# Attention on one Trainium2 core: PSUM as a ring of eight single banks, one exp per head, repeated transfers for the split rows

## The chip, the cores and the metric

The kernel runs on one NeuronCore of a Trainium2 chip. The metric is the device time of one launch in microseconds, from repeated runs; the profile is that of one further execution.

The engines named below are TensorE (PE in the profile; PEld is its weight load), VectorE (DVE), ScalarE (ACT), GpSimd (POOL) and SyncE (SP), whose list here only issues transfers. A transfer is issued by SP, by ACT or by POOL, each in the order of its own list.

## The reference

One transformer block with conditioning, on x of shape 2 x 2048 x 576 in float32, with 16 heads of 36 dimensions and an MLP of 2304:

```python
mod = jax.nn.silu(c) @ w_ada + b_ada
sh_msa, sc_msa, g_msa, sh_mlp, sc_mlp, g_mlp = jnp.split(mod, 6, axis=1)
xn = _ln(x, 1e-06) * (1 + sc_msa[:, None, :]) + sh_msa[:, None, :]
qkv = (xn @ w_qkv + b_qkv).reshape(B, N, 3, H, hd)
q, k, v = (qkv[:, :, 0], qkv[:, :, 1], qkv[:, :, 2])
q = _ln(q, 1e-05, qn_g, qn_b)
k = _ln(k, 1e-05, kn_g, kn_b)
attn = jnp.einsum('bqhd,bkhd->bhqk', q, k) * hd ** (-0.5)
attn = jax.nn.softmax(attn, axis=-1)
o = jnp.einsum('bhqk,bkhd->bqhd', attn, v).reshape(B, N, C) @ w_proj + b_proj
x = x + g_msa[:, None, :] * o
xn2 = _ln(x, 1e-06) * (1 + sc_mlp[:, None, :]) + sh_mlp[:, None, :]
x = x + g_mlp[:, None, :] * (jax.nn.gelu(xn2 @ w1 + b1, approximate=False) @ w2 + b2)
```

## The kernel before

For each of the two batch entries b the kernel first makes q, k and v for 16 tiles of 128 tokens (`inputs`, L360 and L371 the matmuls), normalises q and k per head, and transposes them to feature-major rows: `qo` holds q's five chunks of 128 features (and the first rows of k), `kr` the rest of k. Then comes `attend`, then the projection (`outputs`). After both entries come the two products of the MLP.

`attend` runs over head pairs p (8), query blocks qb of 512 tokens (4) and key groups g (4): 128 steps for each b. A step works on two heads and on two halves of the keys, which makes four row groups of 32 partitions, so that four small matmuls run side by side in TensorE. A head has 36 dimensions, and a row group takes 32: the first 32 ("main", tiles km and qm) go as float32, two passes each, and the last four ("ends", ke and qe) as 16 rows, in which each of the four dimensions stands four times as high and low part[...]. `parted` splits the copies on VectorE into high and low parts (L767, L768), with masks by partition (low and sign).

In a step, `scores` makes two rounds, one for each of two blocks of 128 keys: four main matmul pairs and four ends matmuls (L974) into two PSUM tiles of two banks each, the two heads side by side; then an exp of 128x1024 for each tile (L979) into one of five `pt` buffers. `values` then multiplies the probabilities of the step before with v (L988, 16 matmul records), both heads into one bank, and VectorE moves this sum into `ot` (L1034 for the first key group, L1036 adds the others). v has a column of ones, so one row of the sum is the denominator. So TensorE's order is scores of step n, values of step n - 1, scores of step n + 1, and so on; the loop writes this order out, and VectorE's order is also that of the code.

PSUM has eight banks of 512 float32 per partition. They are one pool of four two-bank tiles (`s_tile`), used in turn by everything. A step of attention takes four for scores and one for the sum, of which the sum uses one bank.

Work that isn't due at once stands in `later`, a list of lists that is popped once a step: `take_q` issues the transfers of q for the next query block at once and splits the ends two steps on; `take_k` does so for the next head pair's keys four steps on; `finish` sends the denominators to memory and back (L1003, L1004), and `divided` takes the reciprocal (L1007), scales (L1008) and sends the head's rows back into `qo` (L1013) three steps on. All of these transfers are on SP's list. `rows_taken` issues, for each of the four row groups, one or two transfers of main rows (L755) and four of the same four rows of ends (L758).

`hooks` places other work at named steps: transposes of the last two token tiles (`last_inputs`) at the first four steps of each b, and for b = 0 the gates and the MLP's modulation from w_ada at steps of p = 0, 1 and 2. `outputs` later loads rows of x through GpSimd's list (L1065) into parts of `kr`, as soon as these are free.

Of the kernel before, what the change touches and what calls it, by code (L numbers as in the profile page):

```python
# [8 lines left out]
F32 = mybir.dt.float32  # L9
F32R = mybir.dt.float32r  # L10
I32 = mybir.dt.int32
AF = mybir.ActivationFunctionType
# [4 lines left out]
P = 128  # L17
# [14 lines left out]
def dit_block(  # L32
# [53 lines left out]
    def s_tile():  # L86
        return psum["s"].tile([P, 2, 512], F32, tag="s", name="s")

    def acc_tile():
        return psum["a"].tile([P, 512], F32, tag="acc", name="acc")  # L90

# [6 lines left out]
    def opened_psum(**bufs):  # L98

        stack = ExitStack()  # L100
        for n, count in bufs.items():
            psum[n] = stack.enter_context(
                tc.tile_pool(name=f"ps_{n}", bufs=count, space=PSUM, reuse_waits="tile")
            )
        return stack.close

    def load_rows(dst, w):

# [65 lines left out]
    def ada_rows(was):  # L174


        ps = s_tile()[:, 0, :PART]
        for k in range(NKC):
            kk = P if k < FULL else 64
            for c in range(4):  # L180
                i, a = divmod(c, 2)
                nc.tensor.matmul(
                    ps[32 * c : 32 * c + 32, :],
                    sil[:kk, k, :],
                    was[i][:kk, k, 256 * a : 256 * a + PART],
                    start=(k == 0),
                    stop=(k == FULL),
                )
        return ps
# [25 lines left out]

    def features(rows, whichs):

        tp = s_tile()[:, 0, :384].rearrange("p (s r) -> p s r", s=3)
        for s in range(3):
            nc.tensor.transpose(tp[:, s, :], rows[:, s * P : (s + 1) * P], ident)  # L220
        for i in range(2):
            for a, chunks in enumerate((slice(0, 2), slice(2, 5))):
                n = chunks.stop - chunks.start
                r0 = 32 * (2 * i + a)
                nc.vector.tensor_copy(mod[:, whichs[i], chunks, :], tp[:, :n, r0 : r0 + B])
# [480 lines left out]
    def block_of_small():  # L706
# [25 lines left out]
        high = kv.tile([P, BLK], F32R, name="high")  # L732

        low_k, low_q, sign_k, sign_q = (kv.tile([P, 1], F32, name=f"part{i}") for i in range(4))
        eights = ident.rearrange("p (r a b) -> p r a b", r=4, a=4)[:, :, 1, :]
        fours = ident.rearrange("p (r a b d) -> p r a b d", r=4, a=4, b=2)[:, :, 0:2, 1, :]
        nc.vector.tensor_reduce(low_k, eights, AX.XY, ALU.add)
        nc.vector.tensor_reduce(low_q, fours, AX.XYZ, ALU.add)
        for low, sign in ((low_k, sign_k), (low_q, sign_q)):
            nc.vector.tensor_scalar(sign, low, -2.0, 1.0, ALU.mult, ALU.add)  # L740
        nc.gpsimd.memset(vv[:, :, :, HD : HD + 1], 1.0)
# [4 lines left out]
            return qo[:, c, cols] if c < NKC else kr[:, c - NKC, cols]  # L746


        def rows_taken(main, ends, halves, first, src, dst):

            for c in halves:
                for h in range(2):
                    r0 = 32 * (2 * c + h)
                    for i, row, d, n in head_rows(first + h * HD, DIMS):
                        nc.sync.dma_start(out=main[r0 + d : r0 + d + n, dst], in_=chunk(i, src(c))[row : row + n, :])  # L755
                    ((i, row, _, n),) = head_rows(first + h * HD + DIMS, HD - DIMS)
                    for j in range(4):
                        nc.sync.dma_start(  # L758
                            out=ends[r0 + n * j : r0 + n * j + n, dst], in_=chunk(i, src(c))[row : row + n, :]
                        )  # L760

        def parted(ends, rows, low, sign):

# [8 lines left out]
        def take_k(p):  # L772
            m, e = km[p % 2], ke[p % 2]
            src = lambda c: slice(c * N // 2, (c + 1) * N // 2)
            rows_taken(m, e, range(2), C + p * 2 * HD, src, slice(0, N // 2))
            return lambda: parted(e, slice(0, P), low_k, sign_k)

        def take_k_block(t0, t1):

            c, k0 = divmod(t0 * P, N // 2)  # L780
            dst = slice(k0, k0 + (t1 - t0) * P)
            rows_taken(km[0], ke[0], (c,), C, lambda c: slice(t0 * P, t1 * P), dst)
            return lambda: parted(ke[0][:, dst], slice(64 * c, 64 * c + 64), low_k, sign_k)

        def take_q(p, qb):
            i = qb % 2
            src = lambda c: slice(qb * BLK, (qb + 1) * BLK)
            rows_taken(qm[i], qe[i], range(2), p * 2 * HD, src, slice(0, BLK))
            return lambda: parted(qe[i], slice(0, P), low_q, sign_q)

        def last_chunk(dst, w, groups, f):
# [35 lines left out]
        def inputs(b, weights, work, xnt, loaded):  # L827
# [64 lines left out]
                    taken.append(take_k_block(*key_tiles[i - 1 : i + 1]))  # L892

            def last(t, chunks):
                ps = s_tile()
                by_feature(t, (ps[:, 0], ps[:, 1]), chunks, True)
                left = [*taken]
                taken.clear()
                return left
# [54 lines left out]
        def attend(b, pool, hooks):  # L954
# [5 lines left out]
            def scores(p, qb, g):  # L960
                i, j = p % 2, qb % 2
                pts = []
                for k0 in (2 * g * P, (2 * g + 1) * P):
                    keys = slice(k0, k0 + P)
                    tiles = [s_tile() for c in range(2)]
                    for k, q, first in (
                        (km[i], qm[j], True),
                        (ke[i].bitcast(F32R), qe[j].bitcast(F32R), False),
                    ):
                        for c in range(2):  # L970
                            for h in range(2):
                                r0 = 32 * (2 * c + h)
                                r = slice(r0, r0 + (DIMS if first else 4 * (HD - DIMS)))
                                nc.tensor.matmul(  # L974
                                    tiles[c][:, h, :], k[r, keys], q[r, :], start=first, stop=not first
                                )
                    for c, ps in enumerate(tiles):
                        pt = pool.tile([P, 2, BLK], F32, name="pt", bufs=5)
                        nc.scalar.activation(pt, ps, AF.Exp, scale=SCALE)  # L979
                        pts.append((pt, k0 // P + c * NT // 2))  # L980
                return pts

            def values(p, pts):
                acc = s_tile()[:, 0, :]
                for pt, kc in pts:
                    for h in range(2):
                        v0 = (kc * H + 2 * p + h) * HV
                        nc.tensor.matmul(  # L988
                            acc[64 * h : 64 * h + 64, :],
                            vt[:, v0 : v0 + 64],  # L990
                            pt[:, h, :],
                            start=pt is pts[0][0],
                            stop=pt is pts[-1][0],
                        )
                return acc
# [27 lines left out]
            for p, qb, g in [*steps, (None, None, None)]:  # L1023
                pts = None if p is None else scores(p, qb, g)
                if g == 0 and (p, qb) != (NPAIR - 1, NBLK - 1):
                    later[2].append(take_q(*((p, qb + 1) if qb + 1 < NBLK else (p + 1, 0))))
                if g == 1 and qb == 1 and p + 1 < NPAIR:
                    later[4].append(take_k(p + 1))
                if behind is not None:
                    bp, bqb, bg, bpts = behind  # L1030
                    acc = values(bp, bpts)
                    if bg == 0:
                        ot = pool.tile([P, BLK], F32, name="ot", bufs=2)
                        nc.vector.tensor_copy(ot, acc)  # L1034
                    else:
                        nc.vector.tensor_tensor(ot, acc, ot, ALU.add)  # L1036
                    if bg == NG - 1:
                        later[3].append(finish(bp, bqb, ot))
                if (p, qb, g) in hooks:
                    later[1] += hooks[p, qb, g]() or []  # L1040
                later.append([])
                for do in later.pop(0):
                    do()
                behind = (p, qb, g, pts)
# [82 lines left out]
        for b in range(B):  # L1127
# [2 lines left out]
                last_inputs = inputs(b, weights, work, xnt, loaded)  # L1130
            close_weights()
            att, close_att = opened("att")
            km[1] = att.tile([P, N // 2], F32, name="km1")
            qm[1] = att.tile([P, BLK], F32, name="qm1")
            opening = {}
# [22 lines left out]
            def output_opened():  # L1158
# [2 lines left out]
            hooks = {  # L1161
                (0, 0, 0): lambda: last_inputs(NT - 2, range(NKC - 1, NQK)),
                (0, 0, 1): lambda: last_inputs(NT - 1, range(NKC - 1, NQK)),
                (0, 0, 2): lambda: last_inputs(NT - 2, range(NKC - 1)),
                (0, 0, 3): last_inputs_done,
                (4, 0, 1): output_opened,
            }
            if b == 0:
# [6 lines left out]
            with tc.manual_schedule(engines={mybir.EngineType.DVE}):  # L1175
                attend(b, att, hooks)
            close_att()
            wp, close_wp = opening["wp"]
            if b + 1 < B:
                weights, close_weights = input_weights()  # L1180
# [351 lines left out]
```

## Time and profile before

| | |
|---|---|
| median of 3 runs | 3327.55 us (3326.79 to 3329.52) |
| the profiled execution | 3329.74 us, of which span 3327.5 us |
| granted TensorE clock | 0.994 |
| TensorE busy | 3250.7 us (98%) |
| ScalarE busy | 1440.7 us (43%) |
| VectorE busy | 1457.9 us (44%) |
| GpSimd busy | 255.0 us (8%) |

By stretches of the span: first conditioning to 30 us; q, k and v of b = 0 to 258 us; attention to 1075 us; projection to 1146 us; q, k, v and attention of b = 1 to 2190 us; projection to 2291 us; first MLP product to 2829 us; second to the end. Between 300 and 1075 us TensorE is busy for 761.56 us, ScalarE for 478.16, VectorE for 258.04 and GpSimd for 24.70.

How to read it: a row of a group gives line, engine, operation, output and input tiles with shapes, the count, then busy time and mean nanoseconds of one, then the idle time of the engine just before and what ended it. A float32 matmul shows as two records. The chain of waits gives start, length and what the end of the program was waiting for at that moment; "issue" is time in which the engine waited for nothing that the profile shows. A timeline line gives start, length, engine, line, operation, tiles and, in brackets, the idle time before it with its releaser; SPq is SP's list of transfers.

### The profile page before, as it was taken

How to read it: one execution, taken by the hardware profiler on the slowest of the kernel's cores; microseconds unless marked ns; L12 is line 12 of the kernel's file. 1: busy time of each engine (PE TensorE's matmuls, PEld its weight loads, DVE VectorE, ACT ScalarE, POOL GpSimd, SP SyncE). 2: the span in 40 equal slices, each digit the busy share in tenths (PEclk: the TensorE clock that was granted, in tenths of full speed). 3: DMA queues.
4: the chain of work that ended last, by engine and by line, in shares of the span. 5: the costliest groups of instructions: out<-in, count | busy, mean ns of one | idle time of the engine just before them, and what ended most of it. 6: DMA issues, size and time to landing. Idle time of an engine off the chain costs nothing.

```text
span 3327.5 us, 47009 instructions
## 1 busy us (share of the span) xinstructions
PE 3250.7 (98%) x18143; PEld 1892.2 (57%) x18143; DVE 1457.9 (44%) x2073; ACT 1440.7 (43%) x1928; POOL 255.0 (8%) x249
## 2 busy tenths in 40 slices
PE   8999999999999999999999999998999999999998
PEld 5774333333333777633333333357888788777776
DVE  4664333333333366533333333255455443554554
ACT  2335656666666033356666666633555543000000
POOL 1110000000000211100000000041000000111111
PEclk9999999999999999999999999999999999999999
DMA  3002212212111401021111111144322222523321
GB/s 127 26 27 62 73 44 64 54 45 52 45 44 29 143 26 30 18 57 44 42 42 43 36 44 41 35 169 145 120 84 88 81 81 77 191 100 119 130 100 37
DMA packets 123324, 234.28 MB, mean 70 GB/s; under 512 B 22412, under 2 KB 65365, under 8 KB 121045
## 3 DMA queue, kind: packets, MB, share of 16 engines
q1 hardware_dynamic: 112124, 193.10, 18.8%
q0 software_dynamic: 10240, 36.61, 3.2%
q8 instruction: 146, 2.39, 0.3%
q10 hardware_dynamic: 728, 1.48, 0.1%
q14 instruction: 86, 0.70, 0.1%
HBM read 125.96 MB, written 56.91 MB: 55 GB/s over the span
## 4 chain that ended last, share of the span: by engine, by line
PE 86%; ACT 7%; issue 2%; DMA 2%; DVE 1%; SPq 1%; POOL 0%; ACTq 0%; DVEq 0%; POOLq 0%
PE s L988 28%; PE s L1460 14%; PE s L360 14%; PE s L974 11%; PE m L1310 11%; ACT pt L979 7%; PE m L1324 2%; PE s L371 2%; PE one L1310 2%; PE s L874 1%; DMA wb<-in_w_dram 1%; PE t L1369 1%; SPq L758 0%; PE s L338 0%; DMA qo<-ot 0%
## 5 line engine op out<-in xcount | busy, mean ns | idle before, releaser
L979 ACT ACTIVATE pt<-s 128x1024 f32<-128x1024 f32 x1024 | 994.1, 1024 | 611.2 <-PE s L988 348.0
L988 PE MATMUL s<-pt,vt 128*64 128x512 f32 x4096 | 940.1, 601 | 18.0
L988 PEld LDWEIGHTS s<-pt,vt 128*64 128x64 f32 x4096 | 272.9, 137 | 621.1 <-issue 452.8
L974 PE MATMUL s<-qm,km 32*128 32x512 f32 x4096 | 578.0, 616 | 5.8 <-DVE ot L1034 5.7
L974 PE MATMUL s<-qe,ke 16*128 16x512 f32 x2048 | 430.9, 789 | 5.2 <-DVE ke L768 4.6
L1036 DVE TENSOR_TENSOR ot<-s,ot 128x512 f32<-128x512 f32 x192 | 132.7, 691 | 682.7 <-PE s L988 682.7
L360 PE MATMUL s<-wq,xnt 128*128 128x288 f32 x1536 | 394.2, 412 | 3.6 <-ACT xnt L346 3.6
L974 PEld LDWEIGHTS s<-qm,km 32*128 32x128 f32 x4096 | 193.5, 185 | 280.1 <-ACT pt L979 203.4
L1460 PE MATMUL s<-ws,as 128*128 128x288 f32 x1440 | 351.8, 406 | 0.0
L360 PEld LDWEIGHTS s<-wq,xnt 128*128 128x128 f32 x1536 | 287.1, 191 | 96.0 <-issue 18.5
L1460 PEld LDWEIGHTS s<-ws,as 128*128 128x128 f32 x1440 | 273.6, 190 | 75.6
L1007 DVE RECIPROCAL den<-den 128x512 f32<-128x512 f32 x64 | 213.9, 3343 | 3.8 <-DMA den<-den_dram 3.8
L1310 PE MATMUL m<-xnt,wb 128*128 128x256 f32 x864 | 214.5, 384 | 0.9 <-DVE product L1074 0.9
L1310 PE MATMUL m<-s,wb 128*128 128x256 f32 x864 | 210.2, 379 | 3.1 <-DVE s L1284 3.1
L1034 DVE COPY ot<-s 128x512 f32<-128x512 f32 x64 | 44.2, 691 | 364.6 <-PE s L988 264.3
L974 PEld LDWEIGHTS s<-qe,ke 16*128 16x128 f32 x2048 | 112.0, 185 | 120.6 <-issue 111.9
L1310 PEld LDWEIGHTS m<-s,wb 128*128 128x128 f32 x864 | 164.0, 190 | 26.1 <-DVE s L1284 3.5
L1310 PEld LDWEIGHTS m<-xnt,wb 128*128 128x128 f32 x864 | 159.4, 190 | 33.8 <-issue 12.2
L1337 DVE TENSOR_TENSOR cs<-m,cs 128x512 f32<-128x512 f32 x72 | 49.7, 691 | 233.5 <-ACT cs L1336 157.2
L1460 PE MATMUL s<-ws,hidden 128*128 128x288 f32 x576 | 142.3, 406 | 0.0
L1348 ACT ACTIVATE cs<-cs,b_sb 128x512 f32<-128x512 f32 x144 | 103.9, 722 | 87.4 <-DVE cs L1343 87.4
L1446 DVE TENSOR_TENSOR as<-hidden 128x1152 f32<-128x1152 f32 x80 | 139.5, 1807 | 0.0
(147 smaller groups left out, 2433.2 us busy)
## 6 DMA issues: line engine op xcount, KB each, us to landing
gelu<-cs SPq DMA_DIRECT2D x144, 256.0 KB
hidden<-gelu SPq DMA_DIRECT2D x16, 2304.0 KB
qe<-qo SPq DMA_DIRECT2D x1024, 8.0 KB
den<-den_dram SPq DMA_DIRECT2D x128, 128.0 KB
qm<-qo SPq DMA_DIRECT2D x192, 64.0 KB
xr<-x_dram SPq DMA_DIRECT2D x32, 288.0 KB
out_dram<-y POOLq DMA_DIRECT2D x32, 288.0 KB, 3.7
qo<-ot SPq DMA_DIRECT2D x104, 72.0 KB
```

Source lines behind the costliest of these rows:

```text
L360: nc.tensor.matmul(outs[a], stationary(k, a), moving(k, a), start=(first and k == 0), stop=(not first and k == FULL - 1),)
L371: nc.tensor.matmul(outs[a], stationary(FULL, a)[r], moving(FULL, a)[r], start=first, stop=not first)
L974: nc.tensor.matmul(tiles[c][:, h, :], k[r, keys], q[r, :], start=first, stop=not first)
L979: nc.scalar.activation(pt, ps, AF.Exp, scale=SCALE)
L988: nc.tensor.matmul(acc[64 * h : 64 * h + 64, :], vt[:, v0 : v0 + 64], pt[:, h, :], start=pt is pts[0][0], stop=pt is pts[-1][0],)
L1007: nc.vector.reciprocal(den, den)
L1036: nc.vector.tensor_tensor(ot, acc, ot, ALU.add)
L1310: nc.tensor.matmul(out_m[m], wb[:, slot[m], k, f * P : (f + 1) * P], moving[m](k), start=k == 0 and (m == 1 or (first and m in (2, 5, 6))) ...
L1324: nc.tensor.matmul(out_m[m], w[r, f * P : (f + 1) * P], a[r, FULL, t * PAIR : (t + 1) * PAIR], start=first and m != 4, stop=not first and ...
L1348: nc.scalar.activation(part, part, AF.Gelu, bias=b1_sb[:, g : g + 1])
L1446: nc.vector.tensor_tensor(stationary[m], x_, y_, op)
L1460: nc.tensor.matmul(ms[m], stationary[m][:, f, :], ws[m][:, f, :], start=(f == 0), stop=(f == HF - 1))
```

## The change

In attention, and there alone, PSUM is opened as eight tiles of one bank (`psum["b"]`); `bank()` takes the next of them, or half an `s_tile` where that pool isn't open. Each score matmul group gets a bank of its own and each head an exp of 128x512 into its half of `pt`. The sum takes the ninth bank of a step, which in a ring of eight is the step's first one again.

The four transfers of ends become one whose source repeats each row four times. The copies of a row now lie side by side, not the four rows as blocks, so the masks of the split change. `take_k` issues on GpSimd's list, all else stays on SP's. Two of the four hooks of `last_inputs` move from steps 2 and 3 to steps 4 and 5, and what a hook returns is put ahead of what `later` holds for that step.

```diff
+    def bank():
+        return psum["b"].tile([P, 512], F32, tag="b", name="b") if "b" in psum else s_tile()[:, 0, :]
...
-        eights = ident.rearrange("p (r a b) -> p r a b", r=4, a=4)[:, :, 1, :]
-        fours = ident.rearrange("p (r a b d) -> p r a b d", r=4, a=4, b=2)[:, :, 0:2, 1, :]
-        nc.vector.tensor_reduce(low_k, eights, AX.XY, ALU.add)
-        nc.vector.tensor_reduce(low_q, fours, AX.XYZ, ALU.add)
+        parts = ident.rearrange("p (r a b) -> p r a b", a=2, b=2)
+        nc.vector.tensor_reduce(low_k, parts[:, :, 1, :], AX.XY, ALU.add)
+        nc.vector.tensor_reduce(low_q, parts[:, :, :, 1], AX.XY, ALU.add)
...
-                    for j in range(4):
-                        nc.sync.dma_start(
-                            out=ends[r0 + n * j : r0 + n * j + n, dst], in_=chunk(i, src(c))[row : row + n, :]
-                        )
+                    values = chunk(i, src(c))[row : row + n, :]
+                    queue.dma_start(
+                        out=ends[r0 : r0 + 4 * n, dst],
+                        in_=values.unsqueeze(1).to_broadcast([n, 4, values.shape[1]]),
+                    )
...
-            rows_taken(m, e, range(2), C + p * 2 * HD, src, slice(0, N // 2))
+            rows_taken(nc.gpsimd, m, e, range(2), C + p * 2 * HD, src, slice(0, N // 2))
...
-                    tiles = [s_tile() for c in range(2)]
+                    banks = [bank() for _ in range(4)]
...
-                        for c in range(2):
-                            for h in range(2):
-                                r0 = 32 * (2 * c + h)
-                                r = slice(r0, r0 + (DIMS if first else 4 * (HD - DIMS)))
-                                nc.tensor.matmul(
-                                    tiles[c][:, h, :], k[r, keys], q[r, :], start=first, stop=not first
-                                )
-                    for c, ps in enumerate(tiles):
+                        for r0, ps in zip(range(0, P, 32), banks):
+                            r = slice(r0, r0 + (DIMS if first else 4 * (HD - DIMS)))
+                            nc.tensor.matmul(ps, k[r, keys], q[r, :], start=first, stop=not first)
+                    for c in range(2):
                         pt = pool.tile([P, 2, BLK], F32, name="pt", bufs=5)
-                        nc.scalar.activation(pt, ps, AF.Exp, scale=SCALE)
+                        for h in range(2):
+                            nc.scalar.activation(pt[:, h, :], banks[2 * c + h], AF.Exp, scale=SCALE)
...
-                acc = s_tile()[:, 0, :]
+                acc = bank()
...
-                    later[1] += hooks[p, qb, g]() or []
+                    later[1] = (hooks[p, qb, g]() or []) + later[1]
...
+            close_psum()
+            close_psum = opened_psum(b=8)
...
-                (0, 0, 2): lambda: last_inputs(NT - 2, range(NKC - 1)),
-                (0, 0, 3): last_inputs_done,
+                (0, 1, 0): lambda: last_inputs(NT - 2, range(NKC - 1)),
+                (0, 1, 1): last_inputs_done,
...
             close_att()
+            close_psum()
+            close_psum = opened_psum(s=4)
```

More of the change, by code (lines that the diff above doesn't have):

```diff
@@ L104, in opened_psum, with close @@
             )
-        return stack.close
+        def close():
+            stack.close()
+            for n in bufs:
+                del psum[n]
+        return close
     def load_rows(dst, w):
@@ L174, in ada_rows @@
     def ada_rows(was):
-        ps = s_tile()[:, 0, :PART]
+        ps = bank()[:, :PART]
         for k in range(NKC):
@@ L216, in features @@
     def features(rows, whichs):
-        tp = s_tile()[:, 0, :384].rearrange("p (s r) -> p s r", s=3)
+        tp = bank()[:, :384].rearrange("p (s r) -> p s r", s=3)
         for s in range(3):
@@ L746, in chunk, with rows_taken @@
             return qo[:, c, cols] if c < NKC else kr[:, c - NKC, cols]
-        def rows_taken(main, ends, halves, first, src, dst):
+        def rows_taken(queue, main, ends, halves, first, src, dst):
             for c in halves:
@@ L754, in rows_taken @@
                     for i, row, d, n in head_rows(first + h * HD, DIMS):
-                        nc.sync.dma_start(out=main[r0 + d : r0 + d + n, dst], in_=chunk(i, src(c))[row : row + n, :])
+                        queue.dma_start(out=main[r0 + d : r0 + d + n, dst], in_=chunk(i, src(c))[row : row + n, :])
                     ((i, row, _, n),) = head_rows(first + h * HD + DIMS, HD - DIMS)
-                    for j in range(4):
-                        nc.sync.dma_start(
-                            out=ends[r0 + n * j : r0 + n * j + n, dst], in_=chunk(i, src(c))[row : row + n, :]
-                        )
+                    values = chunk(i, src(c))[row : row + n, :]
[3 more added lines that the diff above has]
+                    )
         def parted(ends, rows, low, sign):
@@ L781, in take_k_block @@
             dst = slice(k0, k0 + (t1 - t0) * P)
-            rows_taken(km[0], ke[0], (c,), C, lambda c: slice(t0 * P, t1 * P), dst)
+            rows_taken(nc.sync, km[0], ke[0], (c,), C, lambda c: slice(t0 * P, t1 * P), dst)
             return lambda: parted(ke[0][:, dst], slice(64 * c, 64 * c + 64), low_k, sign_k)
@@ L787, in take_q @@
             src = lambda c: slice(qb * BLK, (qb + 1) * BLK)
-            rows_taken(qm[i], qe[i], range(2), p * 2 * HD, src, slice(0, BLK))
+            rows_taken(nc.sync, qm[i], qe[i], range(2), p * 2 * HD, src, slice(0, BLK))
             return lambda: parted(qe[i], slice(0, P), low_q, sign_q)
@@ L894, in last @@
             def last(t, chunks):
-                ps = s_tile()
-                by_feature(t, (ps[:, 0], ps[:, 1]), chunks, True)
+                by_feature(t, [bank() for _ in range(0, len(chunks), 4)], chunks, True)
                 left = [*taken]
```

## The prediction

> **What bounds the kernel now.** I read the page first (busy shares, then the chain that ended last), then the rows of the three attention lines, then the chain of waits over a few steps, then the timelines of ScalarE and of SP's queue.
>
> ```profile
> PE 3250.7 (98%) x18143; PEld 1892.2 (57%) x18143; DVE 1457.9 (44%) x2073; ACT 1440.7 (43%) x1928; POOL 255.0 (8%) x249
> PE 86%; ACT 7%; issue 2%; DMA 2%; DVE 1%; SPq 1%; POOL 0%; ACTq 0%; DVEq 0%; POOLq 0%
> L979 ACT ACTIVATE pt<-s 128x1024 f32<-128x1024 f32 x1024 | 994.1, 1024 | 611.2 <-PE s L988 348.0 <-PE s L974 262.3
> L1336 ACT COPY cs<-one 128x256 f32<-128x256 f32 x72 | 26.8, 372 | 172.9 <-PE one L1310 160.5 <-ACT std L265 12.0 <-PE t L1369 0.2
> ```
>
> TensorE counts as busy for 98%, yet the chain that ended last gives ScalarE 7%, all of it in the exps of L979. Ends of matmuls are modelled, so a TensorE that stands still for a fraction of a microsecond can pass for busy. The chain of waits over two attention steps shows where:
>
> ```profile
> 344.28 3.65 PE s L988 x16
> 347.94 1.36 PE s L974 x11
> 349.30 0.00 ACTq L979
> 349.31 0.04 issue
> 349.35 1.03 ACT pt L979
> 350.38 0.04 issue
> 350.43 1.93 PE s L988 x7
> ```
>
> A step (one of 2 x 128) is 3.65 us of L988 (probabilities times values) and two rounds of scores (L974). The next L988 starts only after an exp of 1.03 us. Each step takes five two-bank tiles from a ring of four, so the sum of L988 gets the tile of the step's first score pair, whose exp has just begun. TensorE's timeline, first in this step, then in a step where ScalarE was long done, gives the price:
>
> ```profile
> 349.06 1.04 PE L974 MATMUL s<-qm,km 32*128 32x512 f32 x8
> 349.52 0.81 PE L974 MATMUL s<-qe,ke 16*128 16x512 f32 x4
> 350.43 0.65 PE L988 MATMUL s<-pt,vt 128*64 128x512 f32 x2
> ...
> 1640.54 0.70 PE L974 MATMUL s<-qm,km 32*128 32x512 f32 x2 [0.37 <-DVE ot L1034]
> 1640.55 0.50 PE L974 MATMUL s<-qe,ke 16*128 16x512 f32 x2
> 1641.07 0.59 PE L974 MATMUL s<-qm,km 32*128 32x512 f32 x2
> 1641.10 0.80 PE L974 MATMUL s<-qe,ke 16*128 16x512 f32 x2
> 1641.83 0.65 PE L988 MATMUL s<-pt,vt 128*64 128x512 f32 x2
> ```
>
> From the last "ends" matmuls to L988 it is 0.91 us with the wait and 0.73 us without. Of the 0.17 some 0.03 is the spread of four starts against two, so the exp costs 0.14 us a step, not its whole 1.03.
>
> The second window also shows another wait: L974 waits for DVE's copy into ot (L1034), and that for qo<-ot on SP's queue, which had no free moment before it:
>
> ```profile
> 1624.03 0.54 SPq L755 DMA_DIRECT2D km<-kr  x1
> 1624.61 1.23 SPq L758 DMA_DIRECT2D ke<-kr  x2
> 1625.94 1.80 SPq L755 DMA_DIRECT2D qm<-qo  x3
> 1627.83 7.05 SPq L758 DMA_DIRECT2D qe<-qo  x11
> 1634.98 2.12 SPq L1013 DMA_DIRECT2D qo<-ot  x3
> ```
>
> **The sum wait (each head's exp by itself, sum in the first head's bank).** 1024 exps of 128x1024 become 2048 of 128x512. Their price is not in the trace; the two rows above, PSUM sources at 1024 and 256 elements, give (1024 - 372) / 768 = 0.849 ns an element, so about 590 ns for 512. Three long exps in a row take 2.85 us in ScalarE's timeline, one each 0.91, so neighbours overlap by 0.11: 0.48 us each. The Trainium skill, "ScalarE: Activation LUTs", section "What ACT_TABLE_LOAD costs", states 186 ns plus 0.833 ns an element and an overlap of about 93 ns, so 613 ns and 0.52 us each, which speaks for cutting exps into fewer, longer ones. I take the trace's 0.48 and keep 0.52 as the upper end of the likely.
>
> Does it fit? With five pt buffers, the exps of a step from its third on wait for L988 to free a buffer: the first of them starts 1.19 us after L988 (345.49 or 351.61 in the timeline). Six short exps then end at 1.19 + 5 x 0.48 + 0.59 = 4.18 us (4.40 by the skill's price). Their banks are wanted again by the second round of scores, whose weight loads start at 348.83 - 344.28 = 4.55 and matmuls at 4.78. So it fits by 0.37 or 0.15 us. The sum's bank: its exp starts at 349.35 as before, ends at 349.94 instead of 350.38, and TensorE could take it up at 350.26 at the earliest (349.52 + 0.73). The wait is then hidden by 0.3 us of scores; what is late next is TensorE itself. Gain 0.14 us a step, over the some 230 of 256 steps in which the trace is undisturbed: 32 us. ScalarE's total goes from 4.1 to 4.2 us of a 6.0 us step at most.
>
> **One repeated transfer instead of four.** Each take of q or k issues about 4.75 transfers of main rows and 16 of ends; the ends become 4. The qe issues take 7.05 / 11 = 0.64 us each on SP, so 12 fewer save 7.7 us of SP time per take. A block of four steps (24.6 us) holds about 17.9 us of SP issues in an ordinary stretch (344 to 363: 2.91 + 7.03 + 1.52 + 0.61 + 1.49 + 2.52 + 0.67 + 1.15), and another 13 in the one block per head pair where k is taken, which doesn't fit. Bytes are the same. The price of the repeated transfer is not in the trace: as the four had it at best (0.64 for all, landing 1.63 us as ke<-kr in the chain), as all four in a row at worst (2.6 us), which is no gain. I take the former, since issue time follows the instruction in all these rows (0.54 to 0.8 us for 8 to 128 KB). Low and sign masks change their pattern only: two DVE reductions in set-up, beside DMA, at nothing; without that cover, under 1 us.
>
> **k on GpSimd's queue.** About nine transfers of 0.54 us issue (L1065, two in 1.07 us), 5 us per head pair, on an engine that is 8% busy; landing near 4 us. They pass SP's list of q, den and qo. Behind them on GpSimd stand the memsets for ada and the loads of x for the projection, none due for tens of us; the memsets wait at most for key rows, all written by step 1. Against it speaks "SBUF — State Buffer" in the Trainium skill, section "SBUF: two separate sides": a transfer issued from GpSimd gets no descriptors while DVE holds the port they share. By the trace DVE's longest operation here is the 3.34 us reciprocal (L1007). Were each of nine transfers held by one, it would be 30 us; nothing in the trace says that the reciprocal holds the port. km is free one head pair early, and the split of k on DVE stands nine steps (54 us) behind that: hidden by either price. If it weren't, DVE would stand in its list before an eviction, and TensorE with it.
>
> What the relief of SP is worth: of the 254 gaps between L988 starts most are 6.13 to 6.15 us. Eight, about one per head pair (1.3 us in the window above), are over by 8 in sum; six behind the ada loads (408 to 456 us) by 11. I count 15 of these 19 us, the rest because 18 ada transfers and 2.6 MB of weights stay on SP.
>
> **Start of each half, last rows moved.** The first three gaps of a half are 7.46, 9.89 and 8.31, then 7.45, 10.84 and 8.79 us: 7.2 and 8.7 over. In it TensorE waits for the last keys:
>
> ```profile
> 290.89 0.68 PE L974 MATMUL s<-qe,ke 16*128 16x512 f32 x2 [2.31 <-DVE ke L768]
> 292.94 1.98 PE L988 MATMUL s<-pt,vt 128*64 128x512 f32 x4
> ```
>
> After that pause L988 takes 4.86 us instead of 3.65 (granted clock 0.96 over the stretch). The two heads' keys go through ten transfers (282.13 to 288.6); six fewer and the split placed ahead of q's on DVE bring the keys some 3.7 us earlier, so the 2.3 us pause and most of the 1.2 us behind it go. The transposes of the last q columns only move, from steps 2 and 3 to 4 and 5; with them each half keeps about 2.8 us of transposes. I count 9 of 15.9 us. New pools of PSUM and the close of work two steps later: a handful of waits at the two ends of attention, put at zero, bounds minus and plus 2 us.
>
> **Sum.** 32 + 15 + 9 = 56 us off the profiled execution of 3329.74 us (span 3327.5 and 2.2 around it): 3273.7. That execution stood 2.2 us above the median 3327.55, so 3271.5 by the median; say 3271.
>
> **Rivals.**
> 1. The queue alone (chance 0.18): something other than the exp holds L988, such as a last matmul's drain, and the 0.14 isn't freed. For it: in the row of the wait TensorE counts as busy to within 0.1 us. Against: the 0.73 us in each step without the wait. Then 24 us: 3303.
> 2. More than counted (0.15): weight loads that now stand behind ScalarE's semaphore run early, 0.1 us of the first round too (its halves lie 0.53 us apart, in the second round 0.43). Another 25 us or so: 3246.
> 3. ScalarE becomes the bound, slower (0.07): the short exps don't overlap. Then the sixth ends at 1.19 + 6T, and the second round waits as soon as that passes its matmuls at 4.78; the 0.14 is eaten at T about 0.60. At T = 0.63 (590 plus 0.04 for the semaphore) the round is 0.32 late, net 0.18 us a step, 46 us lost and 24 won: 3350. The nearest 128x512 row, the gelu of L1348 at 722 ns, would give 0.83 us a step, 3517. Against: 3 in 2.85 us shows overlap.
> 4. k late on GpSimd or the transfer as dear as four (0.06): DVE waits in its list and passes it on; with gain 1 kept and 2 gone, 3300, or no change at all if each head pair loses 3 us.
>
> **How the numbers follow.** My case has 0.54. It and rivals 1, 2 and part of 4 lie in 3240 to 3308; the slower case lies outside. A difference of 0.2%, some 7 us, is about what a measurement of this kernel can tell from no change. Faster 0.90, same 0.02, slower 0.08.
>
> **What would show it.** L979 x2048 with a mean near 590 ns; L988 starts 5.98 to 6.0 us apart, with about 0.73 us from the last ends matmuls; ScalarE's share of the chain near 1%; a quarter of the qe issues, no SP stretch without gaps in attention, and no wait of L974 for ke. It is wrong if L974 waits for ScalarE's pt in the second round (rival 3), if gaps stay at 6.13 (rival 1), or if DVE waits for km or ke (rival 4).

## The result, and the profile after

The changed kernel takes 3270.53 us in the median of 4 runs (3265.76 to 3275.02), against 3328.53 us (3326.79 to 3331.43, 4 runs). The ratio is 0.9825, with a 95% interval of 0.9808 to 0.9842. The forecast was 3271. Five later runs of the same program gave 3268.35 us, ratio 0.9820 (0.9807 to 0.9834).

From the page of the changed kernel, the busy shares, the chain that ended last by engine, and the rows of the exps and of the values' matmuls (L985 and L994 are L979 and L988 of before, b is the ring of single banks):

```profile
PE 3218.1 (98%) x18143; PEld 1888.4 (58%) x18143; DVE 1456.7 (45%) x2073; ACT 1504.6 (46%) x2952; POOL 318.0 (10%) x369
PE 95%; DMA 1%; issue 1%; DVE 1%; ACT 0%; POOL 0%; SPq 0%; DVEq 0%; POOLq 0%; ACTq 0%
L985 ACT ACTIVATE pt<-b 128x512 f32<-128x512 f32 x2048 | 1058.0, 610 | 487.2 <-PE b L994 271.1
L994 PE MATMUL b<-pt,vt 128*64 128x512 f32 x4096 | 935.1, 599 | 0.0
```

TensorE's busy share is 98% as before, though 59 us are gone. What moved is the second line: ScalarE's share of the chain fell from 7% to 0, TensorE's rose from 86% to 95%. The share of busy time could not show the wait; the chain could.

The chain of waits over two steps, then TensorE's and ScalarE's timelines of the second one:

```profile
340.85 3.58 PE b L994 x16
344.43 2.41 PE b L981 x23
346.84 3.58 PE b L994 x16
350.42 1.72 PE b L981 x12
...
344.36 1.14 PE L981 MATMUL b<-qm,km 32*128 32x512 f32 x8
344.92 0.82 PE L981 MATMUL b<-qe,ke 16*128 16x512 f32 x4
345.56 1.04 PE L981 MATMUL b<-qm,km 32*128 32x512 f32 x8
346.02 0.82 PE L981 MATMUL b<-qe,ke 16*128 16x512 f32 x4
346.77 3.65 PE L994 MATMUL b<-pt,vt 128*64 128x512 f32 x16
...
341.99 3.04 ACT L985 ACTIVATE pt<-b 128x512 f32<-128x512 f32 x6 [1.07 <-PE b L994]
345.84 1.08 ACT L985 ACTIVATE pt<-b 128x512 f32<-128x512 f32 x2 [0.81 <-PE b L981]
347.95 3.04 ACT L985 ACTIVATE pt<-b 128x512 f32<-128x512 f32 x6 [1.03 <-PE b L994]
```

No exp stands between two sums any more. From the last ends matmuls to L994 it is 0.75 us (346.02 to 346.77) where it was 0.91. The first exp of a pair, at 345.84 with 0.61 us, ends at 346.45 and has freed the sum's bank 0.3 us early. Six exps end 4.22 us after the sum's start (347.95 + 3.04 - 346.77), ahead of the second round's weight loads at about 4.55.

The starts of the sums' matmuls, taken from the timelines, give this account of attention (us over both halves; a gap runs from one sum's start to the next, the quiet gap is the median, and "over" is measured against the quiet gap of the same kernel; the last sum of a half, with no scores ahead of it, is left to the last row but one):

| | before | after | gained | forecast |
|---|---|---|---|---|
| quiet gap, times 252 | 6.1245 | 5.980 | 36.4 | 32 |
| over: first six gaps of each half | 16.1 | 9.6 | 6.5 | 9 |
| over: the nine gaps behind the first ada loads | 11.1 | 0.0 | 11.1 | 15 with the next row |
| over: all later gaps but the gates' and modulation's own matmuls | 9.5 | 1.7 | 7.8 | |
| outside of these gaps | | | -3.0 | 0 |
| span | 3327.5 | 3268.6 | 58.9 | 56 |

The rows miss the span's 58.9 by 0.1 us, which is in the gates' and modulation's matmuls. The 3 us outside are scatter: the same three stretches (up to the first sum, between the halves, behind the last) were 1740.9 us in the profile before, 1743.9 here and 1740.5 in the later profile of the same program.

### The profile page after: what moved, and what is told of

It reads as the page before. It is cut to its first block, busy times and chain, and to the rows that moved or that the text cites. A ratio compares the mean times of both kernels' runs of the same rounds, so it can differ in the third digit from the quotient of the medians.

```text
span 3268.6 us, 46758 instructions
## 1 busy us (share of the span) xinstructions
PE 3218.1 (98%) x18143; PEld 1888.4 (58%) x18143; DVE 1456.7 (45%) x2073; ACT 1504.6 (46%) x2952; POOL 318.0 (10%) x369
## 4 chain that ended last, share of the span: by engine, by line
PE 95%; DMA 1%; issue 1%; DVE 1%; ACT 0%; POOL 0%; SPq 0%; DVEq 0%; POOLq 0%; ACTq 0%
PE b L994 28%; PE b L981 19%; PE s L370 14%; PE s L1470 14%; PE m L1320 12%; PE m L1334 2%; PE s L381 2%; PE one L1320 2%; PE s L884 1%; PE t L1379 1%; DMA wb<-in_w_dram 1%; PE s L348 0%; DMA wq<-in_w_qkv_dram 0%; DVE xt L278 0%; DMA wa<-in_w_ada_dram 0%
## 5 line engine op out<-in xcount | busy, mean ns | idle before, releaser
L985 ACT ACTIVATE pt<-b 128x512 f32<-128x512 f32 x2048 | 1058.0, 610 | 487.2 <-PE b L994 271.1
L994 PE MATMUL b<-pt,vt 128*64 128x512 f32 x4096 | 935.1, 599 | 0.0
L994 PEld LDWEIGHTS b<-pt,vt 128*64 128x64 f32 x4096 | 271.8, 136 | 581.4 <-issue 439.4
L981 PE MATMUL b<-qm,km 32*128 32x512 f32 x4096 | 567.9, 614 | 2.0 <-DVE vt L936 1.6
L1042 DVE TENSOR_TENSOR ot<-b,ot 128x512 f32<-128x512 f32 x192 | 132.7, 691 | 656.2 <-PE b L994 656.2
L981 PE MATMUL b<-qe,ke 16*128 16x512 f32 x2048 | 423.5, 789 | 0.0
L981 PEld LDWEIGHTS b<-qm,km 32*128 32x128 f32 x4096 | 192.4, 185 | 271.8 <-ACT pt L985 206.5
L1040 DVE COPY ot<-b 128x512 f32<-128x512 f32 x64 | 44.2, 691 | 339.1 <-PE b L994 321.0
L981 PEld LDWEIGHTS b<-qe,ke 16*128 16x128 f32 x2048 | 108.8, 184 | 114.1 <-issue 112.8
L356 ACT ACTIVATE xnt<-s,mod 128x128 f32<-128x128 f32 x180 | 66.6, 458 | 159.8 <-PE s L349 159.8
```

The source lines that it names most:

```text
L356: nc.scalar.activation(dst[:, k, :], t4[:, k * P : (k + 1) * P] if k < FULL else t1[:, :P], AF.Identity, bias=mod[:, which, k, b : b + 1], ...
L981: nc.tensor.matmul(ps, k[r, keys], q[r, :], start=first, stop=not first)
L985: nc.scalar.activation(pt[:, h, :], banks[2 * c + h], AF.Exp, scale=SCALE)
L994: nc.tensor.matmul(acc[64 * h : 64 * h + 64, :], vt[:, v0 : v0 + 64], pt[:, h, :], start=pt is pts[0][0], stop=pt is pts[-1][0],)
```

## The experiments

**1. The ring alone.** All of the diff but `rows_taken`, the masks and the hooks:

```diff
+                    banks = [bank() for _ in range(4)]
+                            nc.scalar.activation(pt[:, h, :], banks[2 * c + h], AF.Exp, scale=SCALE)
+                acc = bank()
```

> The kernel before with the ring of eight banks and the exps by head alone; transfers, masks, queues and hooks as before. My theory (the sum waited 0.14 us a step for its bank, and SP's list is a second, separate cost): 3293 us, up to 3303 because the shorter steps leave SP less time; starts of the sum's matmuls 5.98 us apart in quiet stretches, the late ones at head pairs and behind the ada loads still there. Rival (the queue alone brought the gain): 3325.

Measured: 3314.86 us, ratio 0.9955 (0.9939 to 0.9972). The quiet gap is 5.98 us, so all of the ring's gain is there; yet only some 14 us reach the end where I expected 35, and the run lies above the 3303 that I gave as the upper end. The timeline of SP's list in this run, at the change of head pairs:

```profile
697.44 2.48 SPq L768 DMA_DIRECT2D ke<-kr  x4
699.97 0.54 SPq L765 DMA_DIRECT2D km<-kr  x1
700.55 1.23 SPq L768 DMA_DIRECT2D ke<-kr  x2
701.88 1.80 SPq L765 DMA_DIRECT2D qm<-qo  x3
703.76 7.05 SPq L768 DMA_DIRECT2D qe<-qo  x11
710.92 1.40 SPq L1019 DMA_DIRECT2D qo<-ot  x2
```

It is the list of before, issue behind issue at the same prices. A head pair's issues take SP the same time whatever TensorE does, so where SP is the bound, shorter steps only turn into waiting: the later gaps were over by 25.8 us in this run against 9.5 before. The table of who waited for whom shows TensorE at it:

```profile
DVE ot L1040 <- DMA qo<-ot: 85.0, 11, 9.6
...
PE b L981 <- DVE ot L1040: 13.5, 11, 3.2
```

Its columns are the sum, the count and the longest, in us. Eleven times VectorE's copy into `ot` (L1040) waits for `qo<-ot`, at the end of SP's list, and eleven times TensorE waits for such a copy. In the kernel before, VectorE's copy waits as often (12 times, 81.9 us), but TensorE only 4 times, for 5.7 us. Another 5 us went between the halves.

**2. The transfers alone.** The kernel before with the repeated transfer, its masks and k on GpSimd's list:

```diff
-                    for j in range(4):
-                        nc.sync.dma_start(out=ends[r0 + n * j : r0 + n * j + n, dst], ...)
+                    queue.dma_start(out=ends[r0 : r0 + 4 * n, dst], in_=values.unsqueeze(1).to_broadcast(...))
...
+            rows_taken(nc.gpsimd, m, e, range(2), C + p * 2 * HD, src, slice(0, N // 2))
```

> The kernel before with the repeated transfer and k on GpSimd's list alone; PSUM, exps and hooks as before. My theory: the late steps go, the wait for the exp stays at 6.13 us a step: 3304 us (20 for the late steps and 4 at the starts). Rival (SP's list was late only because of the ring's waits): 3325.

Measured: 3306.73 us, ratio 0.9932 (0.9915 to 0.9948), as my theory had it. The quiet gap stays at 6.12, the gaps behind the ada loads are over by 0.1 us in place of 11.1, the later ones by 1.9. So SP's list had a cost of its own. Alone the two parts save 14 and 22 us; together, with the hooks, 58 to 61.

**3. The sum's bank, two edits that tested nothing.** One passed over a bank ahead of the sum, the other turned the order of a pair's exps around:

```diff
+                bank()
                 acc = bank()
```

> The changed kernel, but one bank of the ring is passed over before the sum, so that the sum takes the bank of the step's second score group, whose exp ends some 0.48 us later. My theory: the sum waits for that exp again, 1.08 us after the first exp's start plus 0.05: 6.18 us a step, 3320 us. Rival (a drain of TensorE or the switch between the two kinds of matmuls holds the sum, the exp does not): 3270.

```diff
-                        for h in range(2):
+                        for h in (1, 0):
                             nc.scalar.activation(pt[:, h, :], banks[2 * c + h], AF.Exp, scale=SCALE)
```

> The changed kernel with the two exps of each pair in the other order, so that the sum's bank (still the step's first) is read by the second exp. The run with a bank passed over gave the sum the same bank as before, so it tested nothing. My theory: the sum waits for that exp, which ends 1.08 us after the pair's start (345.84 to 346.92 in the timeline of the changed kernel), where it starts now at 346.77: 0.2 us more a step, 6.18 us, 3318 us. Rival (a drain of TensorE or the switch of matmul kinds holds the sum, not the exp): 3270.

They gave 3268.63 us (0.9818, 0.9803 to 0.9835) and 3268.89 us (0.9819, 0.9803 to 0.9834). I read the reason from the built programs: a bank that no instruction uses takes no turn, so the sum got the bank it had before; and ScalarE's order is not that of the code here, so the exp of the first head's bank still came first in the pairs that matter. The traces name no banks, but they agree: in both runs a sum starts before the second exp of the pair ahead of it has ended (344.69 against 344.85 us, and 345.40 against 345.55), so it was not waiting for that one. The two runs say nothing on the theory and stand as repeats of the changed kernel.

**4. The sum's bank held.** One element of the passed-over bank is written, so that it takes its turn:

```diff
-                acc = bank()
+                nc.vector.memset(bank()[0:1, 0:1], 0.0)
+                acc = bank()
```

> The changed kernel with one element of the next bank of the ring zeroed by VectorE ahead of the sum in every step (a bank that is only passed over is taken again at once, and the exps' order is set by the readiness of their matmuls, so that the two earlier runs left the sum in the bank of the first exp). Now the sum gets the bank that the second exp reads. My theory: that exp ends 1.08 us after the pair's start (345.84 to 346.92 in the timeline of the changed kernel), the sum starts 0.05 later instead of at 346.77: 0.2 us more a step, 6.18 us, 3318 us. Rival (the switch of matmul kinds holds the sum, the exp does not): 5.98 us a step and 3270.

Measured: 3311.65 us, ratio 0.9949 (0.9932 to 0.9966). The chain of waits has the exps back in every step (L995 are the values there):

```profile
344.26 3.65 PE b L995 x16
347.91 1.40 PE b L981 x11
349.31 1.07 ACT pt L985 x2
350.39 0.04 issue
350.43 2.79 PE b L995 x11
```

The sums start 6.17 us apart (350.43 - 344.26) instead of 5.98. Beside the short write on VectorE, only the exp that frees the sum's bank differs, and the chain names it: it is the exp that holds the sum. The 0.19 us a step give back 43 of the 60 us. The rival of a drain or a switch of matmul kinds is out, for neither is changed here.

**5. ScalarE's margin.** The exps' bias, and then the scale as well, come from tiles that hold the same constants:

```diff
-                            nc.scalar.activation(pt[:, h, :], banks[2 * c + h], AF.Exp, scale=SCALE)
+                            nc.scalar.activation(pt[:, h, :], banks[2 * c + h], AF.Exp, bias=zero, scale=SCALE)
```

> The changed kernel with the exps' bias read from a tile of zeros, which changes no value; each exp gets about 0.09 us longer (two such operands make a 128x128 row 0.34 us from start to start, against 0.16 us by the short exps' slope), so about 0.57 us from start to start. My theory: the sixth exp ends 4.73 us after the sum's start, 0.06 us ahead of the second round's matmuls: 3270 to 3296 us. Rival (ScalarE is 46% busy and has no bearing): 3270.

```diff
+                            nc.scalar.activation(pt[:, h, :], banks[2 * c + h], AF.Exp, bias=zero, scale=by)
```

> As the run with one operand read from a tile, but the scale too: about 0.66 us from start to start, 5.3 us of exps in a step of 6 us, still below TensorE's time. My theory: the sixth exp ends 5.28 us after the sum's start, the second round of scores is late by about 0.5 us in every step: 3380 to 3430 us, slower than before. Rival (only the sum of busy time counts, and it still fits): 3270 to 3280.

Measured: 3298.43 us, ratio 0.9909 (0.9890 to 0.9928), 2 us above the upper end of what I expected; and 3429.45 us, ratio 1.0304 (1.0284 to 1.0323), at its upper end. Rows and timelines, first of the one, then of the other (lines 987 and 983, then 989, 985 and 998, are the exps, the scores and the values there):

```profile
L987 ACT ACTIVATE pt<-b,zero 128x512 f32<-128x512 f32 x2048 | 1240.4, 692 | 336.4 <-PE b L996 255.1
...
346.49 3.58 ACT L987 ACTIVATE pt<-b,zero 128x512 f32<-128x512 f32 x6 [1.01 <-PE b L996]
...
350.55 0.58 PE L983 MATMUL b<-qm,km 32*128 32x512 f32 x1
...
350.65 0.59 PE L983 MATMUL b<-qm,km 32*128 32x512 f32 x1
...
345.31 5.47 ACT L989 ACTIVATE pt<-b,zero,by 128x512 f32<-128x512 f32 x8 [1.21 <-PE b L998]
...
348.88 1.30 PE L985 MATMUL b<-qm,km 32*128 32x512 f32 x7
...
350.02 0.59 PE L985 MATMUL b<-qm,km 32*128 32x512 f32 x1
350.05 0.80 PE L985 MATMUL b<-qe,ke 16*128 16x512 f32 x1
350.78 3.65 PE L998 MATMUL b<-pt,vt 128*64 128x512 f32 x16
```

With one operand the exps start (3.58 - 0.69) / 5 = 0.58 us apart, and the last main matmul of the second round, whose bank the step's last exp reads, comes 0.10 us behind the others: that exp ends at 346.49 + 3.58 = 350.07, and the straggler's weights are loaded only then. The gap is 6.11. With two, eight exps in 5.47 us are 0.67 apart, the straggler is at 350.02, and the gap is 6.65. ScalarE has then 5.4 us of exps in a step that took 5.98: it fits in sum, and still costs 159 us, because six of the eight can't start before the sum has freed a `pt` buffer. The price goes up steeply: the first 0.09 us an exp cost 0.13 us a step, the next 0.09 cost 0.54.

**6. k's queue.** k back on SP's list, in two runs, the second beside the unedited changed kernel:

```diff
-            rows_taken(nc.gpsimd, m, e, range(2), C + p * 2 * HD, src, slice(0, N // 2))
+            rows_taken(nc.sync, m, e, range(2), C + p * 2 * HD, src, slice(0, N // 2))
```

> The changed kernel with k's transfers back on SP's list. My theory: with repeated transfers SP has some 10 us of issues in a block of 24 us and 6 more where k is taken, so it fits: 3270 to 3274 us. Rival (GpSimd's list is what freed SP): the late step per head pair is back, 3277 to 3280.

> The changed kernel unedited, to stand beside the next run on one chip: 3270 us by either theory.

> The changed kernel with k's transfers on SP's list, a second time with more rounds. If k's place is without weight: the same as the run beside it to 2 us. If transfers issued by GpSimd cost something (a later start of each head pair): 3 to 4 us less than it.

Measured: 3266.44 us (0.9809, 0.9792 to 0.9825), then 3266.58 us (0.9813, 0.9800 to 0.9826) beside 3268.35 us (0.9820, 0.9807 to 0.9834). The later gaps are over by 0.5 and 0.3 us against 1.7 in both runs of the changed kernel. The move to GpSimd gains nothing; the 1.8 us less without it are within the intervals.

**7. Four transfers again, with their masks, k on GpSimd.**

```diff
-                    queue.dma_start(out=ends[r0 : r0 + 4 * n, dst], in_=values.unsqueeze(1).to_broadcast(...))
+                    for j in range(4):
+                        queue.dma_start(out=ends[r0 + n * j : r0 + n * j + n, dst], ...)
```

> The changed kernel with four transfers of ends instead of a repeated one; k stays on GpSimd's list. My theory: without k SP has 17.9 us of issues in a block of 23.9 us, which fits outside the ada stretch: 3272 to 3280 us, with late steps behind the ada loads alone. Rival (the count of transfers is what matters): late steps in every head pair, 3287 to 3290.

Measured: 3290.62 us, ratio 0.9882 (0.9863 to 0.9900): the rival's figure and outside of mine, though a late step in every head pair is not there. The later gaps are over by 6.3 us instead of 1.7, and 2.2 of that is one step (331.4 to 339.6 us) in which TensorE waits for a copy into `ot` and that for `qo<-ot`, at the end of SP's list behind the first ada loads. So SP can nearly do without k, as I thought. What I had left out are the starts of the halves: 19.4 us over instead of 9.6, for the last keys' transfers stay on SP. The chain of waits there (in part):

```profile
281.40 0.62 SPq L768
...
283.36 0.74 SPq L768
284.09 0.04 issue
284.13 0.79 SPq L765
...
284.97 0.60 SPq L768
...
286.50 0.66 SPq L768
...
287.20 1.70 DMA ke<-kr
...
289.51 0.49 DVE ke L778
...
290.04 2.74 PE b L981 x11
```

SP issues the copies of the last keys one by one (281.4 to 287.2), and TensorE waits for the split. In the changed kernel this stretch of the chain is TensorE's alone. Another 4 us went between the halves and 4 behind the last sum; why is open.

**8. The hooks back.**

```diff
+                (0, 0, 2): lambda: last_inputs(NT - 2, range(NKC - 1)),
+                (0, 0, 3): last_inputs_done,
...
+                    later[1] += hooks[p, qb, g]() or []
```

> The changed kernel with the transposes of the last q columns back at steps 2 and 3 and the old order of what is due. My theory: the first steps of each half lose some of the pause for the last keys' ends again, 1 to 2 us per half: 3272 to 3275 us. Rival (the move is what shortened the starts): 3277 and more.

Measured: 3272.61 us, ratio 0.9832 (0.9814 to 0.9850). In the trace the first six gaps of the halves are 15.1 us over against 9.6, with VectorE in the chain again:

```profile
285.49 1.36 DVE qo L893 x4
286.85 0.41 DVE high L777
...
287.28 0.76 DVE qe L778
...
288.46 0.50 DVE ke L778
...
289.00 2.77 PE b L981 x12
```

The moved transposes' evictions (qo) and q's split stand ahead of k's split. So the move shortens the starts by 5.5 us in the trace, which is what the rival said, while the time is the one I expected: 2 to 4 us above the other runs of the changed kernel, which the intervals don't tell from nothing.

## Why the prediction was right, point by point

- **What bounds the kernel.** Right: the sum waited for its bank's exp, shown by experiments 1 and 4, and SP's list was a second bound, shown by 1 and 2. TensorE itself is late next: no step of attention waits for ScalarE.
- **The sum wait.** 0.14 us a step was right (6.12 to 5.98). I multiplied it with 230 steps and not with all, so 32 stands against 36.4.
- **Price of a short exp.** Forecast 590 ns and 0.48 us from start to start; measured 610 and (3.04 - 0.61) / 5 = 0.49. Of the two estimates from the Trainium skill ("ScalarE: Activation LUTs", "What ACT_TABLE_LOAD costs"), 613 ns is the better length and 0.52 us the worse interval: it gives an overlap of about 93 ns, and here neighbours overlap by 0.12 us. Its price for an operand from a tile, about 93 ns, is what experiment 5 gave (0.49, 0.58 and 0.67 us from start to start).
- **ScalarE as the bound (rival 3).** The mechanism is real, in the round of scores I named. I put the point at which the ring's gain is eaten at about 0.60 us; experiment 5 reaches it at 0.58, so the changed kernel stands 0.09 us an exp away. The working behind it does not hold, though. By its own formula and its 4.78 us, waiting only begins at 0.60 (1.19 + 6 x 0.60 = 4.79), and at 0.63 the round would be 0.19 us late, not 0.32; the 0.83 us for 722 ns does not come out of it either. And what waits is not the matmul at 4.78 but the weight load ahead of it, due from 4.55: with one operand the sixth exp ends 4.77 us after the sum's start, and the whole gain is gone.
- **SP's list.** I counted 15 of 19 us and kept 4 for the ada loads; all of those went (11.1 to 0.0). This term was too small, 15 against 18.9. The issue of a repeated transfer was put at 0.64 us.

In SP's timeline of the changed kernel it is a bit more, and GpSimd's takes k at the price forecast:

```profile
340.62 2.90 SPq L764 DMA_DIRECT2D qm<-qo  x4
343.57 2.13 SPq L767 DMA_DIRECT2D qe<-qo  x3
...
366.75 0.52 POOL L764 DMA_DIRECT2D km<-kr  x1
367.33 0.60 POOL L767 DMA_DIRECT2D ke<-kr  x1
```

That is 0.71 us a repeated transfer for three in a row, and 0.5 to 0.6 us for GpSimd's issues.

- **k on GpSimd's queue.** No wait of VectorE for km or ke is left in the table of waits, as forecast. But the transfers of ke took 6.4 us in the median from issue to landing and 8.5 at the longest, not near 4; whether VectorE's operations held them up is open, and nothing waited for them. And the prediction did not ask whether SP needed the relief once its transfers were a quarter: it didn't (experiment 6).
- **Start of each half.** Too large: 9 against 6.5. The pause for the last keys went, as forecast, and it took both parts: with the old hooks the starts are 15.1 us over, with four transfers 19.4. But the first two steps of a half keep 1.5 and 1.1 to 1.4 us over the quiet gap, and the moved transposes 1.0 each, more than the 0.6 us that they take.
- **Rivals 1 and 2.** The queue alone is refuted by experiments 1 and 4. Nothing came on top either: the halves of the first round still lie further apart (344.36 to 344.92 from main to ends, 0.56) than those of the second (345.56 to 346.02, 0.46), as before.

So the sum was right to 3 us by terms of which two were 4 us too small and one 2.5 too large, beside 3 us of scatter: how near it came is partly luck. So is the half microsecond between 3271 and the median, for the profiled execution was forecast at 3273.7 and took 3270.42.

What the prediction didn't say is that its terms don't add up one by one. It gave the ring 32 us and the queue 24; alone the ring brings 14. Had the change been the ring alone, the same working would have missed by some 18 us.

## What to carry to other kernels

Where the bound engine shows 98% busy, read the chain: an exp in it between two matmuls was a wait of 0.14 us that no busy share shows. Before you shorten a step, ask which list runs at its own pace beside it; a queue of many small transfers takes the gain back until it is shortened too. Splitting work for an earlier release costs margin on the engine that now does twice as many instructions, and six of its eight here had to fit into a window, not into the step.

## What was not expected of the hardware

A step in which ScalarE's exps sum to 5.4 us and TensorE's work to 5.98 us took 6.65 us: what decides is the window that the buffers leave. And shorter steps left SP's time as it was, with 25.8 us of late gaps in place of 9.5.

A wait of TensorE also cost more than its length. In the kernel before, the sum behind the wait for the last keys took 4.86 us instead of 3.65, with a granted clock of 0.73 from 292.9 to 297.8 us; the 0.96 that the prediction gives is the mean over 42 us (258 to 300). The sum at 448.29 us, behind a wait for `ot`, took 5.72 us, with a granted clock of 0.50 from 446 to 452. There are three such slow sums in that trace, which lose 5.0 us, six in that of the ring alone, which lose 10.1, and none in that of the changed kernel.
